# Seven products for eight in the Silu stages of a transformer block with a mixture of experts

## The chip, the cores and the metric

One core of one Trainium2 chip runs the whole kernel in fp32. The metric is the time of one execution on the device, in microseconds (us). TensorE (PE) multiplies, with its weight loads shown apart (PEld); VectorE (DVE), ScalarE (ACT) and GpSimd (POOL) do the elementwise work; SyncE (SP) mostly issues DMAs.

## The reference

x has 16 batches of 512 tokens with 256 features. It is normalized, and three terms are added to it: linear attention, a shared expert, and routed experts (two of eight a token, from one of two groups).

```python
xn = layernorm(x)                                   # no scale, no shift
# attention: q, k = elu(xn @ W + b) + 1; kv = k^T v per head; out = (q kv) / (q sum(k)) @ Wo + bo
# shared expert, HIDDEN = 512:
a, b = split(xn @ w_in.T, 2)                        # 256 -> 2 * 512
shared = (silu(a) * b) @ w_out.T
# routed experts share the first layer:
a, b = split(xn @ w1.T, 2)
h = silu(a) * b
routed = sum(h * weight[:, e] @ w2[e].T for e in range(8))   # two of the weights are not zero
out = x + attention + shared + routed
```

Each Silu stage, w1 for the routed experts and w_in for the shared one, is thus a product of 512 tokens x 256 features by 256 x 1024 for every batch.

## The kernel before, in words

The kernel is written in a framework that orders the instructions of each engine itself: a planner takes them by their place in the program and by the times it expects, so an engine's order may differ from the program's, except where `keep_in_program_order` or `issue_after` bind it. On the chip each engine then takes its instructions in that fixed order and waits on semaphores. The framework also assigns the buffers of a pool: `ps_mm` has six PSUM buffers of one bank (128 x 512 fp32), shared by everything with the tag "mm"; `ps_y` has two.

The first part loops over the 16 batches. Iteration b does, in program order:

- `front(b + 1)`: `residual` (POOL, x plus bias into `res`), `project` (PE: `pk`, `pq`; DVE and ACT: feature maps with Exp, tiles `km`, `qm`), `route` (many small DVE operations; `wins` and `ahead_of` on POOL).
- `summarize(b)`: PE `pxk`, an ACT copy to `xk`.
- `normalize(b + 2)`: DVE statistics, an ACT Sqrt (`sd`), DVE scaling to `xn`; `xn` goes to DRAM and comes back in blocks that DVE transposes into `xnT`, features on partitions, tokens along the free axis. Its statistics and Sqrt run ahead of the program's place when x has landed. `load_x(b + 3)` follows.
- `hidden_rows(b)`: the w1 stage. For each of four tiles of 128 tokens it multiplies the tokens (stationary) by the two halves of w1 (moving, 512 columns each), over two chunks of 128 features: 16 matmuls into eight PSUM tiles `phr`. ACT makes Silu of the first half (`sa_hr`), DVE multiplies it by the second (`hr`), SP stores the rows to `h_d` in DRAM.
- `key_sum(b + 1)` (POOL, one PE product `pks`) and `attend(b + 1)` (DVE operations on 1024 elements; SP stores and reloads q).
- `hidden(b)`: the w_in stage, transposed: weights are stationary, 512 tokens move. Four blocks of hidden features, two halves, two chunks: 16 matmuls into `phs`, then Silu and product into `hs_all`.
- `mix(b)` (PE `pvk`, DVE `vk`, PE `pm`, ACT copy `kvo`) and `gather(b)`: per token tile, four products of `hs_all` with `wout_sb` and two of `qT` with `kvo` (`po`, in `ps_y`), added to `res` and stored beside the h row in `h_d`.
- `load_expert`: two of the 16 slots of `w2_sb` an iteration, four DMAs of 128 KB each, on SP. All are loaded after eight batches.

In the last iteration hidden_rows comes first, and the steps of `order()` (the sorting of tokens by pair of experts) are placed between its tiles by `between`. Then the second part starts: for each pair of tiles, `rows()` gathers 2 x 128 rows of `h_d` by an indirect DMA on POOL, `turn()` transposes them (12 ACT copies `hb` and seven DVE transposes a pair; the first two pairs are placed behind instructions that `hidden` returns in `made`), `sums()` multiplies by the two experts of the pair, picked by a register offset into `w2_sb` (`py`), scales, adds, and stores by an indirect DMA.

[...]

Of the kernel before, what the change touches and what calls it, by code (L numbers as in the profile page):

```python
# [10 lines left out]
FP = mybir.dt.float32  # L11
AF = mybir.ActivationFunctionType
ALU = mybir.AluOpType
AX = mybir.AxisListType

P = 128
# [5 lines left out]
def block_kernel(  # L22
# [111 lines left out]
    KR = D + E + G  # L134
    wkr_sb = wp.tile([P, KD, KR], FP)
    nc.scalar.dma_start(out=wkr_sb[:, :, 0:D], in_=wk.rearrange("(p c) f -> p c f", p=P))
# [17 lines left out]
    if B > 1:  # L154
        xs[1] = load_x(1)
    w1_sb = wp.tile([P, KD, 2 * HID], FP)
    nc.sync.dma_start(out=w1_sb, in_=w1.rearrange("(p c) f -> p c f", p=P))
    win_sb = wp.tile([P, KD, 2 * HID], FP)
    nc.sync.dma_start(out=win_sb, in_=w_in.rearrange("(p c) f -> p c f", p=P))
    wv_sb = wp.tile([P, KD, D], FP)  # L160
# [11 lines left out]
    nc.sync.dma_start(out=wout_sb, in_=w_out.rearrange("(c p) d -> p c d", p=P))  # L172
    w2_sb = wp.tile([P, KH, G * NL * D], FP)

# [250 lines left out]
    def hidden_rows(b, xnT, then):  # L425

        for t in range(NT):
            halves = []
            for half in range(2):
                ph = ps_mm.tile([P, HID], FP, tag="mm", name=f"phr_{b}_{t}_{half}")  # L430
                for k in range(KD):
                    nc.tensor.matmul(  # L432
                        ph, lhsT=xnT[:, k, ts(t, P)], rhs=w1_sb[:, k, ts(half, HID)],
                        start=(k == 0), stop=(k == KD - 1),
                    )
                halves.append(ph)
            sa = work.tile([P, HID], FP, tag="sa", name=f"sa_hr_{b}_{t}")
            nc.scalar.activation(sa, halves[0], AF.Silu)  # L438
            hr = work.tile([P, HID], FP, tag="hr", name=f"hr_{b}_{t}", bufs=3)
            nc.vector.tensor_tensor(hr, halves[1], sa, ALU.mult)  # L440
            nc.sync.dma_start(out=h_d[ts(b * NT + t, P), 0:HID], in_=hr)
            between(b, then(t))

    def hidden(b, xnT):

        h = hs_all
        made = []
        for f in range(KH):
            halves = []
            for half in range(2):  # L450
                ph = ps_mm.tile([P, S], FP, tag="mm", name=f"phs_{b}_{f}_{half}")
                for k in range(KD):
                    nc.tensor.matmul(  # L453
                        ph, lhsT=win_sb[:, k, ts(half * KH + f, P)], rhs=xnT[:, k, :],
                        start=(k == 0), stop=(k == KD - 1),
                    )
                halves.append(ph)
            sa = work.tile([P, S], FP, tag="sa", name=f"sa_hs_{b}_{f}")
            made.append((
                nc.scalar.activation(sa, halves[0], AF.Silu),  # L460
                nc.vector.tensor_tensor(h[:, f, :], halves[1], sa, ALU.mult),  # L461
            ))
        return h, made
# [315 lines left out]
    fronts = {0: front(0, normed[0][1])}  # L779
    normed[1] = normalize(1)  # L780
    queries = {}
    xs[2] = load_x(2)
    for b in range(B):
# [22 lines left out]
        if b + 1 < B:  # L806
            hidden_rows(b, xnT, {2: 1}.get)
        ksb, (qT, turned) = sums, queries.pop(b)
# [6 lines left out]
        if b + 1 == B:  # L815
            for w in tiles[:AHEAD]:
                w.rows()
        hs, made = hidden(b, xnT)
        kvo = mix(b, xk, ksb)
# [39 lines left out]
    for half, queue in enumerate((nc.sync, nc.scalar)):  # L859
        far = work.tile([P, 2, D], FP, tag="hr", name=f"far_{half}", bufs=3)  # L860
        queue.dma_start(
# [40 lines left out]
```

## Time and profile before

| | |
|---|---|
| median of 3 runs | 1073.27 us (1071.79 to 1078.44) |
| profiled execution, its own time | 1071.43 us |
| its span, first to last instruction | 1069.6 us |
| granted TensorE clock | 1.000 |
| period of a middle batch | 50.77 us |
| first product of the routed part (`py`) starts at | 823.24 us |
| PE, DVE, ACT, POOL busy | 1052.6, 658.6, 375.7, 239.0 us |

A line of a group reads: line of the kernel, engine, operation, output and inputs by the program's names, shapes, count | busy us, mean ns of one | idle us of that engine just before them, and what ended the idle time. A line of a timeline has start and length in us, then engine, line and operation, and in square brackets the idle time ahead of it with what ended it. The durations of successive matmuls overlap, so their pitch is read from the start of one group to the start of the next.

### The profile page before, as it was taken

The page shows a single profiled execution, that of the slowest core. Times are in us where ns is not written, and L with a number is a line of the kernel's source. Part 1 is how long each engine was busy: PE and PEld are TensorE (multiplying, and loading weights), DVE is VectorE, ACT ScalarE, POOL GpSimd, SP SyncE. Part 2 cuts the span into 40 slices and gives each one's busy share as a digit, 9 for nine tenths or more (in the row PEclk, how much of TensorE's full clock was granted, in tenths as well). Part 3 has the DMA queues.
Part 4 walks back from the last instruction along what each step waited for, and adds up shares of the span by engine and source line. Part 5 has one row for each costly group of instructions (what it writes and reads, how often), then busy time and mean ns, then how long its engine had stood idle before and what let it go on. Part 6 is the DMA issues. An engine that isn't in the chain of part 4 may idle for free. (4 is left out here: it accounts for less than half of the span.)

```text
span 1069.6 us, 11317 instructions
## 1 busy us (share of the span) xinstructions
PE 1052.6 (98%) x3404; PEld 626.0 (59%) x3404; DVE 658.6 (62%) x1744; ACT 375.7 (35%) x703; POOL 239.0 (22%) x307
## 2 busy tenths in 40 slices
PE   7999999999999999999999999999999999999997
PEld 5574847475756666575757484757464444444445
DVE  6957466564647474747474655646864666666662
ACT  3413232223222231313131322212106676677760
POOL 6102111020202020201011110102003555555551
PEclk9999999999999999999999999999999999999999
DMA  7343342423324242423232313031213444554531
GB/s 232 99 119 119 80 137 60 138 81 117 116 88 139 66 135 68 139 60 99 70 108 60 117 42 119 21 117 39 81 50 128 137 151 148 155 152 146 155 123 64
DMA packets 129118, 114.18 MB, mean 107 GB/s; under 512 B 72045, under 2 KB 114045, under 8 KB 128800
## 3 DMA queue, kind: packets, MB, share of 16 engines
q1 hardware_dynamic: 119104, 77.16, 24.0%
q0 software_dynamic: 8976, 35.22, 10.8%
q10 hardware_dynamic: 976, 1.05, 0.3%
q8 instruction: 29, 0.48, 0.2%
q14 instruction: 33, 0.27, 0.1%
HBM read 63.52 MB, written 50.27 MB: 106 GB/s over the span
## 5 line engine op out<-in xcount | busy, mean ns | idle before, releaser
L747 PE MATMUL py<-w_sb,hT 128*128 x536 | 230.3, 592 | 0.2 <-ACT hb L718 0.2
L432 PE MATMUL phr<-w_sb,xnT 128*128 128x512 f32 x512 | 223.3, 593 | 0.0
L453 PE MATMUL phs<-xnT,win_sb 128*128 128x512 f32 x512 | 222.3, 592 | 0.0
L747 PEld LDWEIGHTS py<-w_sb,hT 128*128 128x128 f32 x536 | 101.8, 190 | 128.3 <-issue 127.7
L453 PEld LDWEIGHTS phs<-xnT,win_sb 128*128 128x128 f32 x512 | 97.3, 190 | 115.6 <-issue 112.2
L432 PEld LDWEIGHTS phr<-w_sb,xnT 128*128 128x128 f32 x512 | 96.9, 190 | 113.7 <-issue 105.2
L294 POOL TENSOR_TENSOR res<-x_all,bo_sb 128x1024 f32<-128x1024 f32 x16 | 38.8, 2428 | 435.3 <-DMA h_d<-res 324.0
L547 PE MATMUL po<-wout_sb,hs_all 128*128 128x256 f32 x512 | 123.4, 379 | 1.9 <-DVEq L845 1.9
L547 PEld LDWEIGHTS po<-wout_sb,hs_all 128*128 128x128 f32 x512 | 96.0, 190 | 15.1 <-issue 2.7
L461 DVE TENSOR_TENSOR hs_all<-phs,sa_hs 128x512 f32<-128x512 f32 x64 | 43.4, 681 | 93.5 <-PE phs L453 82.3
L556 DVE TENSOR_TENSOR res<-po,res 128x256 f32<-128x256 f32 x60 | 25.5, 424 | 116.4 <-PE po L547 116.4
L460 ACT ACTIVATE sa_hs<-phs 128x512 f32<-128x512 f32 x64 | 38.2, 597 | 147.9 <-PE phs L453 138.2
L760 POOL DMA_INDIRECT out<-y,goal x67 | 67.8, 1012 | 97.6 <-DVE y L757 87.6
L440 DVE TENSOR_TENSOR hr<-phr,sa_hr 128x512 f32<-128x512 f32 x64 | 43.8, 684 | 58.0 <-PE phr L432 32.7
L303 ACT ACTIVATE km<-km 128x1024 f32<-128x1024 f32 x16 | 16.9, 1057 | 175.4 <-DVE km L302 175.4
L438 ACT ACTIVATE sa_hr<-phr 128x512 f32<-128x512 f32 x64 | 38.0, 597 | 112.2 <-PE phr L432 103.5
L547 PE MATMUL po<-kvo,qT 128*128 128x256 f32 x256 | 66.8, 383 | 0.0
L314 PE MATMUL pk<-wkr_sb,xnT 128*128 128x266 f32 x256 | 61.6, 394 | 0.0
L481 PE MATMUL pxk<-kk_all,xn_all 128*128 128x256 f32 x256 | 57.9, 379 | 0.0
L325 PE MATMUL pq<-wq_sb,xnT 128*128 128x256 f32 x256 | 57.8, 379 | 0.0
L468 POOL TENSOR_TENSOR k<-kk_all 128x512 f32<-128x512 f32 x16 | 27.6, 1722 | 123.6 <-DVE sm L360 122.2
L314 PEld LDWEIGHTS pk<-wkr_sb,xnT 128*128 128x128 f32 x256 | 49.5, 194 | 9.0
(155 smaller groups left out, 1255.1 us busy)
## 6 DMA issues: line engine op xcount, KB each, us to landing
h_d<-hr SPq DMA_DIRECT2D x64, 256.0 KB, 2.5
q_d<-qq_all SPq DMA_DIRECT2D x16, 512.0 KB, 2.8
qb<-q_d SPq DMA_DIRECT2D x64, 128.0 KB, 2.6
w_sb<-in_w SPq DMA_DIRECT2D x64, 128.0 KB, 3.6
h_d<-res SPq DMA_DIRECT2D x60, 129.0 KB, 2.0
x_all<-in_x SPq DMA_DIRECT2D x15, 512.0 KB, 4.1
xn_d<-xn_all SPq DMA_DIRECT2D x14, 512.0 KB, 3.1
xb<-xn_d SPq DMA_DIRECT2D x56, 128.0 KB, 3.1
```

The costliest lines, as they stand in the source:

```text
L294: nc.gpsimd.tensor_tensor(res[:, :, 0:D], xs.pop(b), bo_sb.unsqueeze(1).to_broadcast([P, NT, D]), ALU.add)
L314: nc.tensor.matmul(pk, lhsT=xnT[:, k, ts(t, P)], rhs=wkr_sb[:, k, :], start=(k == 0), stop=(k == KD - 1),)
L325: nc.tensor.matmul(pq[:, t, :], lhsT=xnT[:, k, ts(t2 + t, P)], rhs=wq_sb[:, k, :], start=(k == 0), stop=(k == KD - 1),)
L432: nc.tensor.matmul(ph, lhsT=xnT[:, k, ts(t, P)], rhs=w1_sb[:, k, ts(half, HID)], start=(k == 0), stop=(k == KD - 1),)
L440: nc.vector.tensor_tensor(hr, halves[1], sa, ALU.mult)
L453: nc.tensor.matmul(ph, lhsT=win_sb[:, k, ts(half * KH + f, P)], rhs=xnT[:, k, :], start=(k == 0), stop=(k == KD - 1),)
L460: nc.scalar.activation(sa, halves[0], AF.Silu),
L461: nc.vector.tensor_tensor(h[:, f, :], halves[1], sa, ALU.mult),
L481: nc.tensor.matmul(pxk[:, c, :], lhsT=xn[:, t, ts(c, P)], rhs=kk[:, t, :], start=(t == 0), stop=(t == NT - 1),)
L547: nc.tensor.matmul(po, lhsT=a, rhs=w, start=(i == 0), stop=(i == len(parts) - 1))
L747: nc.tensor.matmul(py.rearrange("p j d -> p (j d)"), lhsT=self.hT[:, f, ts(j, P)], rhs=w2_sb[:, f, bass.ds(regs[i % TR], 2 * D)], start=(f ...
L760: stored = nc.gpsimd.indirect_dma_start(out=out_rows, out_offset=bass.IndirectOffsetOnAxis(ap=self.goal[:, i : i + 1], axis=0), in_=y, in_ ...
```

## The change

Both Silu stages are rewritten. Tokens and weights are cut in two each, as are the 256 features: x11, x12, x21, x22 (half m of the tokens, half k of the features) and w11, w12, w21, w22. The four blocks of the result, each a sum of two products before, come from seven products of sums of blocks (Winograd's form of Strassen's product). Four sums of token blocks are made per batch on POOL (`token_sums`, shared by both stages), and four differences of weight blocks once per weight on POOL (`weight_sums`).

`seven` runs the products in an order written out by hand, for two units u (two tiles of 128 tokens in `hidden_rows`, two pairs of feature blocks in `hidden`). A unit has three PSUM tiles. In `tall` the sums grow: M1, then M1 + M6, then M1 + M6 + M7, then M4 onto it; ACT copies the first three out between (r1, r2, b2), and DVE adds `lone` (M2) or `wide` (M5, then M3 onto it) to the copies. The results are Silu(r1) times r2 for the first half of the tokens, and Silu of the finished `tall` times b2 for the second. A product is one matmul of 512 columns in `hidden_rows` and two of 256 in `hidden`.

Beside it: the w1 blocks and wq lie in four expert slots of `w2_sb` (12 to 15), which are loaded only after the last `hidden_rows`; w1 and w_in come in three DMAs each; `hr` has four buffers for three; the first turns of the routed part hang on `made[0]` and `made[1]`, the second halves of the two units, for `made[1]` and `made[3]` before; the steps of `order()` in the last batch come after products 3, 6, 10 and 13.

```diff
+    def spare(i, n=1):
+        first = (LATE + 2 * (i % 2)) * D
+        return w2_sb[:, i // 2, first : first + n * HID]
...
-    wq_sb = wp.tile([P, KD, D], FP)
+    wq_sb = spare(7).rearrange("p (c f) -> p c f", c=KD)
...
+    w1_in = [spare(i) for i in range(SEVEN)]
+    win_sb = wp.tile([P, SEVEN, HID], FP)
+    win_in = [win_sb[:, i, :] for i in range(SEVEN)]
...
+        nc.sync.dma_start(out=left, in_=rows[:, :, 0:HID])
+        nc.sync.dma_start(out=corner, in_=rows[:, 0, HID:])
+        nc.sync.dma_start(out=blocks[2], in_=rows[:, 1, HID:])
...
+    def weight_sums(blocks, w12):
+        w11, w21, w22, t1, t2, t3, t4 = blocks
+        for to, p, m in ((t1, w12, w11), (t2, w22, t1), (t3, w22, w12), (t4, w21, t2)):
+            nc.gpsimd.tensor_tensor(to, p, m, ALU.subtract)
+    def token_sums(b, xnT):
+        x11, x12, x21, x22 = (xnT[:, k, ts(m, S // 2)] for m in range(2) for k in range(KD))
+        ss = one.tile([P, 4, S // 2], FP, tag="ss", name=f"ss_{b}")
+        s1, s2, s3, s4 = (ss[:, i, :] for i in range(4))
+        nc.gpsimd.tensor_tensor(s1, x21, x22, ALU.add)
+        nc.gpsimd.tensor_tensor(s2, s1, x11, ALU.subtract)
+        nc.gpsimd.tensor_tensor(s3, x11, x21, ALU.subtract)
+        nc.gpsimd.tensor_tensor(s4, x12, s2, ALU.subtract)
+        return [x11, x12, s4, x22, s1, s2, s3]
+    def seven(b, name, product, first, second, room, done):
...
+        for n, (u, i) in enumerate((
+            (0, 1), (0, 5), (0, 6), (1, 1), (0, 7), (1, 5), (1, 6), (0, 2), (1, 7), (0, 3), (0, 4),
+            (1, 2), (1, 3), (1, 4),
+        )):
+            to = lone[u] if i == 2 else wide[u] if i in (3, 5) else tall[u]
+            product(to, u, i - 1, i in (1, 2, 5), i in (2, 3, 4))
+            if i == 1:
+                r1[u] = work.tile([P, HID], FP, tag="sa", name=f"r1_{names[u]}")
+                nc.scalar.copy(r1[u], tall[u])
+            elif i == 6:
+                r2[u] = room(u, 0)
+                nc.scalar.copy(r2[u], first(tall[u]))
+            elif i == 7:
+                b2[u] = room(u, 1)
+                nc.scalar.copy(b2[u], first(tall[u]))
+                nc.vector.tensor_tensor(b2[u], b2[u], first(wide[u]), ALU.add)
+            elif i == 2:
+                nc.vector.tensor_tensor(r1[u], r1[u], lone[u], ALU.add)
+                nc.scalar.activation(r1[u], r1[u], AF.Silu)
+            elif i == 3:
+                nc.vector.tensor_tensor(r2[u], r2[u], first(wide[u]), ALU.add)
+                done(u, 0, None, nc.vector.tensor_tensor(r2[u], first(r1[u]), r2[u], ALU.mult))
+            elif i == 4:
+                sa = work.tile([P, HID], FP, tag="sa", name=f"sa_{names[u]}")
+                silu = nc.scalar.activation(sa, tall[u], AF.Silu)
+                done(u, 1, silu, nc.vector.tensor_tensor(b2[u], first(sa), b2[u], ALU.mult))
+            second(n)
...
+            nc.tensor.matmul(to, lhsT=xs7[i][:, ts(u, P)], rhs=w1_in[W7[i]], start=start, stop=stop, skip_group_check=True)
...
+            for f in range(2):
+                tc.keep_in_program_order(nc.tensor.matmul(
+                    split(to)[:, f, :], lhsT=win_in[W7[i]][:, ts(2 * u + f, P)], rhs=xs7[i],
+                    start=start and f == 0, stop=stop, skip_group_check=True,
+                ))
...
     normed[1] = normalize(1)
+    weight_sums(w1_in, w1_12)
...
         if b + 1 == B:
-            hidden_rows(b, xnT, dict.fromkeys(range(NT), 2).get)
+            sums7 = token_sums(b, xnT)
+            hidden_rows(b, sums7, {3: 2, 6: 2, 10: 2, 13: 2}.get)
+            for e in waiting:
+                load_expert(e)
...
+            weight_sums(win_in, win_12)
...
-            hidden_rows(b, xnT, {2: 1}.get)
+            sums7 = token_sums(b, xnT)
+            hidden_rows(b, sums7, {9: 1}.get)
...
-        for e in waiting[: 2 if b + 1 < B else G * NL]:
-            load_expert(e)
-        waiting = waiting[2:]
+        for e in [e for e in waiting[:2] if e < LATE]:
+            load_expert(waiting.pop(0))
...
-        w.turn(made[2 * i + 1])
+        w.turn(made[i])
```

More of the change, by code (lines that the diff above doesn't have):

```diff
@@ L135, in block_kernel @@
     wkr_sb = wp.tile([P, KD, KR], FP)
+    w2_sb = wp.tile([P, KH, G * NL * D], FP)
+    LATE = G * NL - 4
+    def spare(i, n=1):
+        first = (LATE + 2 * (i % 2)) * D
+        return w2_sb[:, i // 2, first : first + n * HID]
     nc.scalar.dma_start(out=wkr_sb[:, :, 0:D], in_=wk.rearrange("(p c) f -> p c f", p=P))
@@ L155, in block_kernel @@
         xs[1] = load_x(1)
[L156 to L159, printed above, removed]
+    SEVEN = 7
+    w1_in = [spare(i) for i in range(SEVEN)]
+    win_sb = wp.tile([P, SEVEN, HID], FP)
+    win_in = [win_sb[:, i, :] for i in range(SEVEN)]
+    w1_12, win_12 = (w2_sb[:, i, 0:HID] for i in range(2))
+    for w, left, blocks, corner in (
+        (w1, spare(0, 2).rearrange("p (c f) -> p c f", c=KD), w1_in, w1_12),
+        (w_in, win_sb[:, 0:KD, :], win_in, win_12),
+    ):
+        rows = w.rearrange("(p c) f -> p c f", p=P)
+        nc.sync.dma_start(out=left, in_=rows[:, :, 0:HID])
+        nc.sync.dma_start(out=corner, in_=rows[:, 0, HID:])
+        nc.sync.dma_start(out=blocks[2], in_=rows[:, 1, HID:])
     wv_sb = wp.tile([P, KD, D], FP)
@@ L172, in block_kernel @@
     nc.sync.dma_start(out=wout_sb, in_=w_out.rearrange("(c p) d -> p c d", p=P))
-    w2_sb = wp.tile([P, KH, G * NL * D], FP)
     def load_expert(i):
@@ L423, in between @@
                 next(steps_of_order)
[L425 to L442, printed above, removed]
@@ L444, in hidden @@
-    def hidden(b, xnT):
+    def weight_sums(blocks, w12):
[11 more added lines that the diff above has]
+        return [x11, x12, s4, x22, s1, s2, s3]
@@ new lines, in seven @@
+    def seven(b, name, product, first, second, room, done):
+        names = [f"{name}_{b}_{u}" for u in range(2)]
+        tall, lone, wide = (
+            [ps_mm.tile([P, HID], FP, tag="mm", name=f"{n}{i}") for n in names] for i in "abc"
+        )
+        r1, r2, b2 = [None] * 2, [None] * 2, [None] * 2
+        for n, (u, i) in enumerate((
[25 more added lines that the diff above has]
+            second(n)
@@ new lines, in hidden_rows, with product, room, done @@
+    def hidden_rows(b, xs7, then):
+        rows = {}
+        def product(to, u, i, start, stop):
+            nc.tensor.matmul(to, lhsT=xs7[i][:, ts(u, P)], rhs=w1_in[W7[i]], start=start, stop=stop, skip_group_check=True)
+        def room(u, half):
+            rows[u, half] = work.tile([P, HID], FP, tag="hr", name=f"hr_{b}_{u}_{half}", bufs=4)
+            return rows[u, half]
+        def done(u, half, silu, product):
+            nc.sync.dma_start(out=h_d[ts(b * NT + 2 * half + u, P), 0:HID], in_=rows[u, half])
+        seven(b, "phr", product, lambda a: a, lambda n: between(b, then(n)), room, done)
@@ L446, in hidden, with split, product, room @@
+    W7 = (0, 1, 2, 6, 3, 4, 5)
+    def hidden(b, xs7):
         h = hs_all
         made = []
[L448 to L462, printed above, removed]
+        def split(a):
+            return a.rearrange("p (f j) -> p f j", f=2)
+        def product(to, u, i, start, stop):
+            for f in range(2):
[3 more added lines that the diff above has]
+                ))
+        def room(u, half):
+            return h[:, 2 * u : 2 * u + 2, ts(half, S // 2)]
+        def done(u, half, silu, product):
+            if half:
+                made.append((silu, product))
+        seven(b, "phs", product, split, lambda n: None, room, done)
@@ L817, in block_kernel @@
                 w.rows()
-        hs, made = hidden(b, xnT)
+        hs, made = hidden(b, sums7)
         kvo = mix(b, xk, ksb)
@@ L859, in block_kernel @@
     for half, queue in enumerate((nc.sync, nc.scalar)):
-        far = work.tile([P, 2, D], FP, tag="hr", name=f"far_{half}", bufs=3)
+        far = work.tile([P, 2, D], FP, tag="hr", name=f"far_{half}", bufs=4)
         queue.dma_start(
```

## The prediction, made before the changed kernel was run

> **What bounds the kernel now.** I read the page first (engine shares, then groups), then the PE timeline of one batch, then busy time by window, then ScalarE, VectorE and GpSimd in the stretches that the change touches.
>
> ```profile
> span 1069.6 us, 11317 instructions
> ...
> PE 1052.6 (98%) x3404; PEld 626.0 (59%) x3404; DVE 658.6 (62%) x1744; ACT 375.7 (35%) x703; POOL 239.0 (22%) x307
> ...
> L432 PE MATMUL phr<-w_sb,xnT 128*128 128x512 f32 x512 | 223.3, 593 | 0.0
> ...
> L453 PE MATMUL phs<-xnT,win_sb 128*128 128x512 f32 x512 | 222.3, 592 | 0.0
> ...
> L440 DVE TENSOR_TENSOR hr<-phr,sa_hr 128x512 f32<-128x512 f32 x64 | 43.8, 684 | 58.0 <-PE phr L432 32.7
> ```
>
> TensorE is busy 98% of the span, and its two groups of Silu products show no idle time ahead of them (last column 0.0). Each group has 512 records, not the 256 matmuls of the program: an fp32 matmul is recorded as two passes. The PE timeline of a middle batch gives the pitch of a pass:
>
> ```profile
> 328.06 3.62 PE L325 MATMUL pq<-wq_sb,xnT 128*128 128x256 f32 x16
> 331.51 3.62 PE L481 MATMUL pxk<-kk_all,xn_all 128*128 128x256 f32 x16
> 334.96 13.90 PE L432 MATMUL phr<-w_sb,xnT 128*128 128x512 f32 x32
> 348.70 0.59 PE L471 MATMUL pks<-k,ones 128*128 128x256 f32 x2
> ```
>
> 32 passes of 512 columns take 348.70 - 334.96 = 13.74 us, 0.429 each, so a 512-column product of the program costs 0.86 us. 16 passes of 256 columns take 331.51 - 328.06 = 3.45 us, 0.2156 each. No bracket with idle time stands behind these rows. The windows show a whole batch, pk to pk:
>
> ```profile
> 324.46:375.23 50.77, 50.77 (x176) 32.26 (x174) 30.21 (x82) 13.50 (x18) 5.95 (x8) 1.00 0.36 104
> ```
>
> Columns: window, length, then busy us of PE, PEld, DVE, ACT, POOL, granted clock, DMA share, GB/s. PE fills all 50.77 us; DVE 30.2, ACT 13.5 and POOL 6.0 have room. So in the fifteen full batches each pass saved is time saved, as long as nothing new makes PE wait. The routed tail (from 823 us, py) is PE-bound too and is not changed.
>
> [...]beside the key sum (485.97 to 487.72) a 4-element VectorE operation takes 1.10 us, and its twin right after it 0.15:
>
> ```profile
> 485.97 1.75 POOL L468 TENSOR_TENSOR k<-kk_all 128x512 f32<-128x512 f32 x1 [4.20 <-DVE sm L360]
> ...
> 486.64 1.10 DVE L366 TENSOR_TENSOR gm<-ex 128x4 f32<-128x4 f32 x1
> 487.67 0.15 DVE L367 TENSOR_TENSOR gm<-ex 128x4 f32<-128x4 f32 x1
> ```
>
> **Passes removed.** hidden_rows: 16 matmuls (32 passes of 512) become 7 x 2 = 14 (28 passes): 13.74 - 28 x 0.4293 = 1.72 us. hidden: 32 passes of 512 become 7 x 2 x 2 matmuls of 256 columns, 56 passes: 13.74 - 56 x 0.2156 = 1.67 us. LDWEIGHTS takes 0.190 and stays below 0.2156, as in pq. Sum 3.38 us a batch, 54.1 us in 16 batches. Against the profiled execution's own 1071.43 us (span 1069.6 and 1.8 around it) that leaves 1017.3 if everything added is hidden. The median of the runs shown, 1073.27, is 0.2% above that execution; I leave this inside the range.
>
> **Work added on the other engines, per batch.** ScalarE: 3 copies per half, 12 in the two stages, at 0.57 (xk, 128x512 from PSUM): 6.8 us, 13.5 becomes 20.3. VectorE: 3 additions per half, 12 x 0.68 (the hr row) = 8.2 us, 30.2 becomes 38.4, 81% of a batch of 47.4. GpSimd: 4 token sums of 128x256 at 0.73 (second key sum): 2.9 us, 6.0 becomes 8.9. No engine becomes the bound by sum; what counts is order.
>
> **The chain inside seven().** M1 is copied out, M6 is added onto it in the same bank, the sum is copied, M7 is added. From the end of a product's pitch: its result is there 0.16 later (592 - 429 ns), ScalarE starts 0.08 after that (Silu at 787.25, passes done at 787.17), copies 0.57, and PE follows about 0.05 later (pm at 821.88 after vk at 821.83): 0.86 us, exactly the one product that is put between. So with ScalarE free the chains of half 0 cost about nothing. The second tight place is product (1,3), which needs b2 of half 1 copied and added: 0.24 + 0.57 + 0.08 + 0.68 + 0.05 = 1.62 us under three products (2.58), but Silu of r1 (0.60) stands ahead of that copy on ScalarE, and the addition and product for r2 of half 0 (2 x 0.68) beside its addition on VectorE. Slack is then below 0.4 us. Before, a pair of products took 3.4 us and used two of the six PSUM buffers, so two more pairs could run ahead of a late reader; now six tiles live at once in the six.
>
> What meets this chain is ScalarE's table changes, from the middle of the rows stage of batch 9:
>
> ```profile
> 487.65 0.57 ACT L486 COPY xk<-pxk 128x512 f32<-128x512 f32 x1
> 488.24 1.28 ACT L438 ACT_TABLE_LOAD   x1
> ...
> 493.22 1.28 ACT L269 ACT_TABLE_LOAD   x1
> 495.09 0.30 ACT L269 ACTIVATE sd<-mv,eps_sb 128x4 f32<-128x4 f32 x1 [0.59 <-DVE mv L267]
> 496.08 1.28 ACT L438 ACT_TABLE_LOAD   x1 [0.69 <-PE phr L432]
> ```
>
> Today the Sqrt of a later batch lies in a gap and blocks ScalarE in order: 1.28 + 0.59 + 0.30 + 1.28 = 3.45 us. Copies need no table, but they queue behind the loads, and PE queues behind the copies. Bounds: 0 if Sqrt falls after b2 of half 1, about 3 us if it falls between two chain copies. Its place is the planner's; I take 0.8 a batch. For VectorE's bursts (attend's operations of 1.2 us at the start of hidden, statistics in the rows stage) against the r2/b2 additions: 0 to 1.2, I take 0.4. Hand-over to the next stage (a PSUM buffer is freed only by the last Silu, 0.16 + 0.08 + 0.60 after the last product, with the 0.43 us key-sum product as cover; then gather waits for the late h of half 1): 0 to 0.9, I take 0.2. Sum 1.4 us x 15 = 21 us.
>
> **One-time edits.** Start: eight weight differences of 128x512 on GpSimd at 1.75 are 14 us; its idle stretches (13.8 to 17.2, 25.4 to 29.1, 35 to 44.8 us) hold most. But VectorE runs without a gap from 25 to 57 us in batch 0, and the additions join that line; if they came last, PE would wait all 8.2 us. Bounds 0 and 10; I take 6. The four late experts wait until the last product of hidden_rows(15) has read w1 in their place: 16 DMAs behind the last row store on SP at 0.41 each are 6.6 us of issue, and 3.6 to 4.6 to land: 11 us, 13 if their 2 MB share the queues with the tile gathers (233 GB/s there). pxk, hidden and mix cover 3.5 + 12.1 + 4; nothing is lost, 4 us if bandwidth fails. The first tile's turn now stands behind the Silu of product (0,4), 9.5 us into hidden instead of 5.4, so its 12 copies (5 us) end near 16.5 where PE is ready at 16: 1 us. Marks of the order on VectorE in the last rows stage: 1 us. End: 2 us. The finer loads of w1 and w_in add four DMA issues of 0.4 us on SP well ahead of their use at 30 us: nothing. wq's new place, four hr buffers: nothing.
>
> **Forecast:** 1017.3 + 21 + 6 + 2 = 1046 us.
>
> **Rivals.**
> The chain hides nearly whole (0.22): the planner sets Sqrt outside the tight places. For it: the order of products is fitted to 0.86 us, and ACT is idle 60% of the time. Against: it must hold 32 times. 1017.3 + 4 at the start + 0.2 x 15 = 1024.
> The 256-column halves run slower than I count (0.06): the page's po row has 123.4/512 = 0.241 a pass. Then 56 x 0.025 x 16 = 23 us come back: 1069. Against: pq and pxk show 0.2156 in a dense run.
> Slower (0.08): ScalarE's in-order queue becomes the bound inside both stages. If a table block of 3.45 us lands on the copy chain and VectorE's burst of 1.2 on the other stage's addition, it is 4.65 x 15 = 70, with 10 at the start and 3 at the end: 1017.3 + 83 = 1100. It decides from (54.1 - 8 + 10.7)/15 = 3.8 us of stall a batch on. Against: the block is that long only when the Sqrt waits for its statistics, and hidden has none where rows has it.
> The likeliest case (0.64) spans 1030 to 1064 by its bounds.
>
> **From these:** about 1% (10.7 us) is what a measurement of this kernel can tell from no change. Faster by more: 0.60 + 0.22 = 0.82; within: 0.04 of the likeliest and the 256-column case, 0.10; slower 0.08. The range 1022 to 1067 leaves out the slow case and part of the 256-column one.
>
> **What would show it.** phr 448 records at 0.43 and phs 896 at 0.216, no other group of PE changed; PE idle rows naming ScalarE copies or VectorE additions at the new products, 0.5 to 2.5 us a batch, most in rows stages with a Sqrt load in them; the batch period 48 to 49 us; routed products starting near 795 to 800 us. I am wrong if the period stays at 50.8, if the phs passes stretch beyond 0.22, if the routed tail first waits for a w2 DMA, or if batch 0 loses more than 10 us.

## The result, and the profile after

The kernel after takes 1079.18 us (median of 10 runs, 1078.17 to 1080.08), the kernel before 1075.30 (10 runs): a ratio of 1.0048, 95% interval 1.0029 to 1.0067. Half a per cent slower, where 1046 was forecast with 1067 as the upper end. The profiled execution took 1079.44 us. Executions of the kernel before range from 1069.9 us at a granted clock of 1.000 to 1078.8 at 0.995, and the profiled one (1071.43) is among the fastest, so the two spans lie 8.0 us apart where the medians lie 3.9 apart. Three lines of its page, then one middle batch by window (columns as before):

```profile
span 1077.6 us, 12384 instructions
...
PE 1025.4 (95%) x3724; PEld 682.5 (63%) x3724; DVE 791.3 (73%) x1936; ACT 470.0 (44%) x883; POOL 310.3 (29%) x379
...
L456 POOL TENSOR_TENSOR ss<-xnT 128x256 f32<-128x256 f32 x16 | 15.0, 937 | 269.0 <-PE phs_1c L534 269.0
```

```profile
233.47:282.21 48.74, 48.41 (x195) 35.40 (x194) 37.28 (x94) 19.08 (x29) 10.05 (x12) 1.00 0.38 109
```

The passes are gone as counted (phr 448 records, phs 896), yet TensorE is now busy 95% of the span, not 98%, and its busy time fell by 27 us only (records of 0.59 us overlap at a pitch of 0.43, so short waits under them count as busy, and so do passes at a halved clock, of which more below). The token sums' row gives the first hint: a sum of 128x256 takes 0.94 us in the mean (0.73 to 1.28), not 0.73, so something lengthens some of them. What TensorE waits for (columns: engine, line, releaser: us in total, times, longest us):

```profile
PE pm L595 <- DVE vk L590: 12.9, 9, 5.1
PE pt L302 <- DVE xn_all L292: 8.6, 2, 8.2
PE phs_0a L534 <- ACT r_phs L483: 6.3, 14, 2.3
PE pk L334 <- DVE qq_all L349: 4.0, 1, 4.0
PE phr_0a L508 <- ACT r_phr L483: 3.9, 1, 3.9
PE phr_1c L508 <- DVE hr L490: 3.2, 1, 3.2
PE phr_0c L508 <- DVE hr L490: 2.2, 5, 0.6
PE phs_1c L534 <- DVE hs_all L490: 1.7, 1, 1.7
```

Before, the same view had only pt (7.8), pm (3.5 in 2) and some 2 us of others. Every new row shown names a reader of the seven products or its neighbour on VectorE.

Where the 62 us went is read from the starts of the stages on TensorE (rows stage of batch b: first phr; routed part: first py). "Ideal" is before minus 3.38 us a batch:

| stretch | before | ideal | after | lost | forecast |
|---|---|---|---|---|---|
| up to rows(1) | 81.2 | 77.8 | 97.2 | 19.4 | 6 |
| rows(1) to rows(14), 13 batches | 659.9 | 616.0 | 645.3 | 29.3 (2.25 each) | 18.2 (1.4 each) |
| rows(14) to py, 2 batches | 82.2 | 75.4 | 87.1 | 11.7 | 4.8 |
| py to the end | 246.4 | 246.4 | 248.0 | 1.6 | 0 |

The losses add up to 62.0 us; 54.1 were saved; the difference is, to 0.1, the 8.0 us between the two spans. The periods are not even: 48.74 us in batches 2 to 6, 53.4 in batch 7, 49.8 to 50.1 in batches 8 to 12; the ideal is 47.38.

**The start.** GpSimd's row and VectorE's beside it:

```profile
17.76 2.37 POOL L314 TENSOR_TENSOR res<-x_all,bo_sb 128x1024 f32<-128x1024 f32 x1
...
21.77 2.34 POOL L314 TENSOR_TENSOR res<-x_all,bo_sb 128x1024 f32<-128x1024 f32 x1
```

```profile
17.84 2.84 DVE L322 TENSOR_SCALAR km<-kk_all 128x1024 f32<-128x1024 f32 x1
...
21.78 2.35 DVE L374 TENSOR_TENSOR ex<-lg,mx 128x8 f32<-128x8 f32 x1
```

km took 0.69 in the kernel before, the 8-element ex 0.16. Now ex ends with the GpSimd instruction beside it (24.13 and 24.11), and km ends 0.55 us behind its own neighbour (20.68 and 20.13), which is less than its 0.69. The author's estimate from these ends is that both waited for the neighbour, rather than ran slowly beside it; by what mechanism was not shown. The residual additions were there before; with the weight differences and token sums GpSimd is busy from 13.9 to 36.5 us without a gap, so VectorE, itself without a gap, loses time again and again: from 28.3 to 35.7 us gm takes 1.10 us, pe 0.72, and four operations of `beats` and `wins` 0.58 to 1.28, where 0.15 to 0.19 is what each takes elsewhere. rows(0) then starts at 37.6 (before 30.5), and lasts longer. Its first copy stands on ScalarE behind a late Exp (ScalarE, then TensorE):

```profile
42.99 1.06 ACT L323 ACTIVATE qm<-qm 128x1024 f32<-128x1024 f32 x1 [3.22 <-DVE qm L322]
43.95 0.22 ACT L378 ACTIVATE ex<-ex 128x40 f32<-128x40 f32 x1
44.08 0.57 ACT L483 COPY r_phr<-phr_0a 128x512 f32<-128x512 f32 x1
```

```profile
44.70 1.26 PE L508 MATMUL phr_0a<-w_sb,ss 128*128 128x512 f32 x2 [3.93 <-ACT r_phr L483]
45.75 1.92 PE L508 MATMUL phr_1c<-w_sb,ss 128*128 128x512 f32 x2
47.45 1.78 PE L508 MATMUL phr_0a<-w_sb,ss 128*128 128x512 f32 x2
```

Bracket: TensorE waits 3.93 us for that copy. The next two products have a pitch of 1.70 and 1.62 us for 0.86. The windows (columns as before) show the granted clock at one half there, and again where the routed part starts:

```profile
45.56:48.97 3.41, 3.41 (x5) 1.33 (x4) 3.41 (x11) 0.58 (x1) 0.00 (x0) 0.50 0.00 0
...
827.21:834.04 6.83, 5.20 (x9) 1.94 (x8) 3.95 (x11) 6.59 (x17) 0.00 (x0) 0.50 0.05 17
```

Three more such stretches of 3.41 us start at 25.08, 62.62 and 776.01. All five come behind waits of TensorE of 2.3 to 5.1 us; in the kernel before none lies between 12 and 1069 us. TensorE was busy for 18.6 of their 20.5 us, so by an estimate from these windows (half of that) up to 9 of the 62 us are lost to the halved clock.

**The end.** pm in batches 14 and 15, and the first routed product:

```profile
776.29 2.05 PE L595 MATMUL pm<-wo_sb,vk 128*128 128x256 f32 x4 [5.06 <-DVE vk L590]
...
826.58 1.43 PE L595 MATMUL pm<-wo_sb,vk 128*128 128x256 f32 x4 [3.69 <-DVE vk L590]
829.63 2.90 PE L831 MATMUL py<-w_sb,hT 128*128 x3 [1.63 <-DMA w_sb<-in_w]
```

Before, the two pm waited 1.82 and 1.71 us. The last row is the late experts' DMAs. The 1.6 us behind py are not this wait: the first 4.4 us of py run at half the clock, in the second of the windows above.

### The profile page after: what moved, and what is told of

Same layout as the page of the kernel before. It is cut to its first block, busy times and chain, and to the rows that moved or that the text cites. A ratio compares the mean times of both kernels' runs of the same rounds, so it can differ in the third digit from the quotient of the medians.

```text
span 1077.6 us, 12384 instructions
## 1 busy us (share of the span) xinstructions
PE 1025.4 (95%) x3724; PEld 682.5 (63%) x3724; DVE 791.3 (73%) x1936; ACT 470.0 (44%) x883; POOL 310.3 (29%) x379
## 5 line engine op out<-in xcount | busy, mean ns | idle before, releaser
L456 POOL TENSOR_TENSOR ss<-xnT 128x256 f32<-128x256 f32 x16 | 15.0, 937 | 269.0 <-PE phs_1c L534 269.0
L323 ACT ACTIVATE km<-km 128x1024 f32<-128x1024 f32 x16 | 16.9, 1058 | 171.5 <-DVE km L322 171.5
L334 PE MATMUL pk<-wkr_sb,xnT 128*128 128x266 f32 x256 | 65.0, 405 | 4.0 <-DVE qq_all L349 4.0
L345 PE MATMUL pq<-w_sb,xnT 128*128 128x256 f32 x256 | 57.8, 379 | 0.0
L631 PEld LDWEIGHTS po<-kvo,qT 128*128 128x128 f32 x256 | 47.5, 190 | 8.9 <-ACT kvo L599 3.0
L345 PEld LDWEIGHTS pq<-w_sb,xnT 128*128 128x128 f32 x256 | 48.6, 190 | 7.0
L565 PEld LDWEIGHTS pxk<-kk_all,xn_all 128*128 128x128 f32 x256 | 48.6, 190 | 6.6
L802 ACT COPY hb<-qq_all 32x256 f32<-32x256 f32 x108 | 43.4, 402 | 17.6 <-DMA qq_all<-h_d,source 12.3
L802 ACT COPY hb<-x_all 32x256 f32<-32x256 f32 (+1 forms) x108 | 42.1, 390 | 14.9 <-DVE hT L814 9.6
L802 ACT COPY hb<-xn_all 32x256 f32<-32x256 f32 x96 | 38.6, 402 | 15.8 <-DMA xn_all<-h_d,source 14.5
L802 ACT COPY hb<-kk_all 32x256 f32<-32x256 f32 x96 | 38.6, 402 | 14.5 <-DMA kk_all<-h_d,source 11.3
```

Source lines behind the costliest of these rows:

```text
L323: nc.scalar.activation(low, low, AF.Exp)
L334: nc.tensor.matmul(pk, lhsT=xnT[:, k, ts(t, P)], rhs=wkr_sb[:, k, :], start=(k == 0), stop=(k == KD - 1),)
L345: nc.tensor.matmul(pq[:, t, :], lhsT=xnT[:, k, ts(t2 + t, P)], rhs=wq_sb[:, k, :], start=(k == 0), stop=(k == KD - 1),)
L456: nc.gpsimd.tensor_tensor(s1, x21, x22, ALU.add)
L565: nc.tensor.matmul(pxk[:, c, :], lhsT=xn[:, t, ts(c, P)], rhs=kk[:, t, :], start=(t == 0), stop=(t == NT - 1),)
L631: nc.tensor.matmul(po, lhsT=a, rhs=w, start=(i == 0), stop=(i == len(parts) - 1))
```

## Experiments

Theory A: the reads of partial sums hold TensorE up, by ScalarE's copies and VectorE's additions. Rival B: what lies on GpSimd (sums and differences) does, through VectorE. Times are medians; "after" is 1079.18. Each kernel was timed beside the kernel before, whose median lay between 1075.3 and 1076.9 in these sessions, and the ratios are to that; a difference from after of less than about 2 us therefore says nothing. The first kernel takes every read away.

```diff
-  copies r1, r2, b2; additions of lone, wide
+  r1 = Silu(lone); r2 = wide * r1; b2 = Silu(tall) * r1
```

> Left out: the three copies and three additions of each half; Silu and the product act on the raw PSUM tiles, so the values are not the reference's. The seven products, token sums and weight differences stay. Theory A (the middle batches lose 1.7 to 2.7 of their 3.38 us to the reads of partial sums, through full ScalarE and VectorE queues): period of a middle batch 47.4 us, rows stage 12.0, hidden 12.1, no stall at pm in batch 14; batch 0 still begins its rows stage near 37.5 us, since the weight differences stay; total 1030 to 1042. Rival B (the loss sits in the hand-over between stages and in the six PSUM tiles, which stay): period above 48.2, total above 1058.

1041.66 us, ratio to before 0.9702 (0.9661 to 0.9743); periods 47.4 to 47.7 (48.6 in batch 7, 48.2 in batch 11), rows(1) at 88.3. So 37.5 us hang on the reads, with the GpSimd work all there: 8.9 up to rows(1), 25.5 in the thirteen middle batches, 4.3 in the last two. A holds for the middle; but it does not say whether the reads cost by their work or by where they stand. At the end the expectation failed. With no addition of partial sums left, pm waits for vk in both last batches all the same:

```profile
738.86 2.04 PE L586 MATMUL pm<-wo_sb,vk 128*128 128x256 f32 x4 [4.71 <-DVE vk L581]
...
789.17 1.25 PE L586 MATMUL pm<-wo_sb,vk 128*128 128x256 f32 x4 [4.14 <-DVE vk L581]
```

From rows(14) to pm it takes 30.7 us, 31.2 before and 33.8 in the kernel after; from rows(15) to pm 35.7, 36.6 and 35.7. In batch 14 VectorE works without a marked gap in the 20 us ahead of vk in all three. So there vk sets the time, passes that TensorE saves ahead of it turn into waiting, and the reads cost 3.1 us in batch 14 and nothing up to pm in batch 15.

**Token sums and buffers.**

```diff
-  ss = the four token sums (GpSimd); return [x11, x12, s4, x22, s1, s2, s3]
+  return [x11, x12, x12, x22, x21, x22, x21]
```

> Left out: the four token sums a batch on GpSimd; raw halves of the tokens stand in their place, so the values are not the reference's. Theory A (they are hidden beside gather): 0 to 4 us below the changed kernel, all of it in batch 0. Rival B [...]: period of a middle batch 0.3 us or more shorter, total 6 us or more below.

1065.09 us (0.9923, 0.9895 to 0.9951), 14.1 less than after. The waits of pm for vk fall from 12.9 us in 9 to 7.8 in 2, so B also has a part. The same with four SBUF buffers under the tag "sa" (two before):

```diff
-  r1[u] = work.tile([P, HID], FP, tag="sa", ...)    # and sa
+  r1[u] = work.tile([P, HID], FP, tag="sa", ..., bufs=4)
```

> As e3, without token sums, and with four SBUF buffers instead of two for r1 and the second Silu, which share a tag. Theory A (the first copy of hidden waits for the last product of rows to free one of the two buffers, and the second Silu for the first product): the wait of 0.2 to 0.4 us before the second product group of hidden goes in every batch, 5 to 8 us below e3. Rival B (PSUM buffers or VectorE's lateness hold the same products): within 2 us of e3.

1058.67 us (0.9863, 0.9821 to 0.9904), 6.4 less again. phs_0a's wait falls from 6.3 us in 14 to at most 0.8. Both were then tried with nothing left out. First the sums are held behind a one-column GpSimd copy of `kvo` of the batch before:

```diff
   kvo = mix(b, xk, ksb)
+  ticks.append(nc.gpsimd.tensor_copy(tick, kvo[:, 0, 0:1]))
...
+  with tc.issue_after(ticks[-1].ins):
       token_sums(...)
```

> The kernel after with one edit: GpSimd's token sums of a batch wait for a small GpSimd copy that reads the mixed weights of the batch before, so that they no longer run beside VectorE's last additions of the shared hidden stage. Nothing is left out. Theory (they cost by where they lie, through the slower VectorE and the later vk): the wait of pm for vk falls from 12.9 us in all to 5 to 8, the middle period from 48.74 to 48.1 to 48.3, and the time to 1067 to 1073 us. Rival (they cost by what they are: the first product of a stage needs them, wherever they lie): PE waits for the token sums instead, the period stays at 48.6 to 48.8, and the time at 1077 to 1080 us.

1070.25 us (0.9961, 0.9946 to 0.9976), 8.9 less; periods of 48.25 in batches 2 to 6, pm's waits 7.8 in 2. What they cost in the kernel after shows where GpSimd and VectorE meet at the end of hidden:

```profile
269.55 1.17 POOL L458 TENSOR_TENSOR ss<-xnT 128x256 f32<-128x256 f32 x1
```

```profile
270.06 1.21 DVE L496 TENSOR_TENSOR hs_all<-r_phs,hs_all 128x512 f32<-128x512 f32 x1
```

L496 takes 0.69 elsewhere. `ss` has one buffer, so the sums can start only when hidden's last product that reads it is done, and that is beside VectorE's last burst; vk comes after that burst, pm after vk. The same kernel once more:

> Once more the kernel with the token sums held, one look (1070.25 us before), to see whether its periods of 48.25 in batches 2 to 6, the 53.4 of batch 7 and the 49.2 after it come again. Theory (the order of issue is fixed in the program): they come again within 0.1 us. Rival (they are a state of the chip): they differ.

The periods came again: 48.25, then 53.4, then 49.2. They belong to the program. Then three buffers under "sa" (the pair sums of the keys share a buffer with `kvo` to make room):

```diff
-  r1[u] = work.tile([P, HID], FP, tag="sa", ...)    # and sa
+  r1[u] = work.tile([P, HID], FP, tag="sa", ..., bufs=3)
...
-  k2 = one.tile([P, 2, D], FP, tag="k2", ...)
+  k2 = one.tile([P, 2, D], FP, tag="kvo", ...)
```

> The kernel after with one edit: the copies of the first partial sums have three SBUF buffers for two; the room comes from the pair sums of the keys, which share a buffer with the mixed weights. Nothing is left out. Theory (the first copy of a stage waits for a buffer that the last product of the stage before still reads): phs_0a's wait of 6.3 us in 14 falls to under 1.5, the middle period to 48.2 to 48.4, the time to 1072 to 1075 us. Rival (the wait moves to the next thing, PSUM's banks or VectorE's additions): the period stays within 0.1 of 48.74 and the time within 2 us of 1079.

1068.09 us (0.9937, 0.9921 to 0.9954), 11.1 less, more than expected; periods 48.11 in batches 2 to 6, 48.6 to 49.3 later. The first copy of hidden, in the kernel after and then with three buffers:

```profile
258.21 0.58 ACT L483 COPY r_phs<-phs_0a 128x512 f32<-128x512 f32 x1 [1.17 <-DVE hr L496]
```

```profile
253.21 0.59 ACT L483 COPY r_phs<-phs_0a 128x512 f32<-128x512 f32 x1 [0.84 <-PE phs_0a L534]
```

The copy had waited for VectorE (the last reader of its buffer); with a third buffer it waits only for its product.

**The start and the end.** The raw quarters of the weights are loaded in place of the eight differences:

```diff
+  for to, k in zip(blocks[3:], (0, 1, 0, 1)):
+      nc.sync.dma_start(out=to, in_=rows[:, k, HID:])
...
-  weight_sums(w1_in, w1_12)
-  weight_sums(win_in, win_12)
```

> Left out: the eight weight differences on GpSimd; four more DMAs a weight put raw quarters in their place, so the values are not the reference's. Theory A (at the start [...]every operation of the first front waits): rows of batch 0 begin at 30 to 32 us instead of 37.6, total 6 to 10 us below the changed kernel. Rival B (the start is lost to the copies queued behind Exp on ScalarE and to VectorE's own queue in batch 0): rows still begin by 32 or earlier but batch 0 ends as late, total at most 3 us lower; or rows begin near 37 and nothing changes.

1071.60 us (0.9976, 0.9962 to 0.9990): rows(0) at 34.7, later than expected, and rows(1) at 88.5, 8.7 us earlier. The differences are near half of the start's loss; the reads, with 8.9 us in the first run, are near the other half. Then eight products in batch 0, with the differences written after it in the program, away from VectorE's first work (`eight_rows` and `eight` are the loops of the kernel before):

```diff
-  hidden_rows(b, sums7, ...); hidden(b, sums7)
+  eight_rows(b, xnT, w1_12, ...); eight(b, xnT, win_12)     # b == 0
...
   gather(b, ...)
+  if b == 0: weight_sums(w1_in, w1_12); weight_sums(win_in, win_12)
```

> Batch 0 keeps the eight products of before; the weight differences come after batch 0's gather, and the first experts are loaded from batch 1 on. Theory A (19 us are lost at the start: [...]batch 0's own queues delay the copies): rows of batch 0 at 30 to 31 us, rows of batch 1 at 81 to 84 us instead of 97, total 11 to 16 us below the changed kernel. Rival B (the 14 us of GpSimd work and the added VectorE work only move into batch 1 and cost the same there): rows of batch 2 no earlier than 140 us (146.5 in the changed kernel), total at most 6 us lower.

1083.86 us (1.0075, 1.0049 to 1.0101), a miss: nothing bound the differences, so the planner placed them at 13.5 to 30 us all the same, and the periods of batches 4 to 7 were 50.1 to 51.2. Eight products in batches 14 and 15 (w12 remade from a difference), alone and then with the former:

```diff
+  if b == 14: nc.gpsimd.tensor_tensor(t1, t1, w11, ALU.add)     # for w1 and w_in
-  hidden_rows(b, sums7, ...); hidden(b, sums7)
+  eight_rows(b, xnT, w1_in[3], ...); eight(b, xnT, win_in[3])   # b >= 14
```

> Batches 14 and 15 use the eight products of before; w12 is made again on GpSimd as t1 + w11. The late experts stay where they are. Theory A (in batches 14 and 15 VectorE is full of the marks of the order, and its additions come late): from the rows stage of batch 14 to the first routed product 82 to 84 us instead of 87, total 3 to 6 us below the changed kernel. Rival B (the late loads of four experts and the gathers set the start of the routed part): the stretch stays at 86 or more and the first routed product waits for a DMA.

> e5 and e6 together: seven products in batches 1 to 13 alone. If start and end are separate losses the gains add: 14 to 22 us below the changed kernel, 1057 to 1065 us, about 10 to 18 below the kernel before. Rival: the start's and the end's work meets the middle and less than half of that remains.

1075.04 us (0.9995, 0.9978 to 1.0011), 4.1 less than after; rows(14) to py 85.0 for 87.1. At the end eight products are faster than seven. Both ends: 1082.16 (1.0069, 1.0046 to 1.0092), a miss too, since the misplaced start stays in it. These with three buffers and held token sums:

> e7, with three SBUF buffers instead of two for r1 and the second Silu (the key sum's tile shares kvo's), and the token sums on GpSimd held back until kvo of the batch before is there, so that they don't run beside VectorE's burst at the end of hidden. Theory A ([...]the first copy of hidden waits for a buffer): a middle batch takes 47.6 to 48.2 us instead of 48.7 to 49.9, total 10 to 18 us below e7. Rival B (the middle's loss is the reads' own work on VectorE): within 5 us of e7.

1060.64 us (0.9859, 0.9828 to 0.9889). Now the start of the first-batch run with the differences bound:

```diff
+  held = nc.gpsimd.tensor_copy(tick0, hs[:, KH - 1, 0:1])       # b == 0
+  with tc.issue_after(held.ins):
       weight_sums(w1_in, w1_12); weight_sums(win_in, win_12)
-  waiting = list(range(G * NL))
+  waiting = [*range(2, LATE), 0, 1, *range(LATE, G * NL)]
```

> The kernel after with eight products in batch 0, as in the run of the first batch's eight products before, but now the eight weight differences are held behind a GpSimd copy that reads the hidden rows of batch 0, so that they cannot be issued in the first 40 us; experts 2 and 3 are loaded in batch 0, experts 0 and 1 last, so that the pace of loads is that of the kernel after. Theory (the start is lost to the differences beside VectorE's work, plus the late copies of the first seven-product stage): the first rows start at 31 to 33 us (after 37.6, before 30.5), batch 1's at 82 to 85 (after 97.2), the periods from batch 2 on stay at 48.7, the differences cost batch 0 or 1 up to 3 us, and the kernel takes 1066 to 1071 us. Rival (what is late at the start comes from the loads and from token sums, or the differences cost as much wherever they lie): batch 2's rows start no earlier than 143 us (after 146.5), and the time is 1076 to 1080 us.

rows(0) at 32.4, rows(1) at 83.7, rows(2) at 134.9 (after 146.5): the start behaved as the theory said, 13.5 us were won by rows(1). Yet the time is 1080.67 (1.0073, 1.0047 to 1.0100), not 1066 to 1071: batches 1 to 6 now take 51.2 us each, batch 7 52.7, and by rows(8) all is lost again. Products and sizes are the same as in the kernel after; the order on VectorE is not. Batch 4, GpSimd, VectorE, TensorE:

```profile
238.56 2.40 POOL L314 TENSOR_TENSOR res<-x_all,bo_sb 128x1024 f32<-128x1024 f32 x1
```

```profile
238.67 2.33 DVE L399 TENSOR_TENSOR beats<-pe 128x24 f32<-128x24 f32 x1
...
246.40 0.68 DVE L490 TENSOR_TENSOR hr<-hr,phr_0c 128x512 f32<-128x512 f32 x1
```

```profile
247.22 1.10 PE L508 MATMUL phr_0c<-w_sb,ss 128*128 128x512 f32 x2 [1.69 <-DVE hr L490]
```

and the same addition and product in the kernel after, a batch with a period of 48.74:

```profile
250.97 0.67 DVE L490 TENSOR_TENSOR hr<-hr,phr_0c 128x512 f32<-128x512 f32 x1
```

```profile
252.01 1.02 PE L508 MATMUL phr_0c<-w_sb,ss 128*128 128x512 f32 x2
```

L490 reads the first wide sum (M5) out of its bank, before the product M3 may be added onto it. On VectorE it stands behind the routing chain of the next batch, 22 small instructions. In the kernel after, the copy that L490 needs ends 1.7 us before L490 starts; TensorE comes 1.04 us behind L490's start and has 0.3 us to spare. In this run GpSimd's residual addition began 0.1 us ahead of the chain's first instruction with two SBUF inputs, `beats`, which took 2.33 us, not 0.17; L490 comes 9.1 us behind the start of rows, not 7.0, and TensorE waits. (The q transpose, 1.23 us, stands ahead of L490 in both.) In the kernel after the same addition runs at 250.34, beside L490 and L492, which read PSUM: both keep their 0.67 us. (From batch 8 on, in the kernel after, the statistics of a later batch, 1.6 us, stand in that chain in place of the transpose, and L490 starts as early, at 6.9; but phr_0c comes one product earlier there, and waits 0.4.)

To test this the chain from `beats` on is held behind `vk` of the batch before, in that kernel and in the kernel after (`ranks` is the part of `route` from `pf` on, batches 1 to 13):

```diff
   kvo = mix(b, xk, ksb)
+  with tc.issue_after(vk_instruction.ins):
+      ranks(b + 1, ...)
```

> The run with held weight differences (1080.7 us) with one more edit: the ranks and marks of routing of the next batch (from beats on, some 25 small VectorE instructions and GpSimd's few) wait until VectorE has made vk of this batch, when VectorE has gaps; nothing is left out. Theory (TensorE's second use of the first wide bank waits for an addition that stands behind this chain on VectorE): the wait phr_0c for hr of 13.8 us in 12 goes to under 2, the periods of batches 1 to 7 fall from 51.2 to 48.5 to 49.2, and the time to 1060 to 1066 us. Rival (the loads of the experts or GpSimd's place set the 51.2): the periods stay above 50.5 and the time above 1076.

> The kernel after with one edit, the ranks and marks of routing held behind vk of the batch before. Theory: the period, 48.74 in batches 2 to 6 and 49.85 to 53.4 from batch 7 on, becomes 48.3 to 48.8 throughout, and the time 1065 to 1071 us; the start stays late (batch 1's rows at 94 to 98 us). Rival: the later batches are slow for another reason, the periods from batch 7 on stay near 49.9, the time within 3 us of 1079.

With held differences: the wait is gone, the periods of batches 1 to 6 are 48.7 to 49.2 for 51.2, as the theory said. But the time is 1074.17 (0.9993), not 1060 to 1066. What took its place:

```profile
PE phs_0a L540 <- ACT r_phs L489: 9.4, 13, 1.4
...
PE po L679 <- DVE res L688: 5.5, 1, 5.5
PE pm L643 <- DVE beats L405: 5.2, 8, 1.0
```

In batch 0 batch 1's chain now meets the weight differences, and seven instructions with two SBUF inputs in a row take 1.12 to 1.30 us each beside them (the next two of the same lines, behind the last difference, 0.18 and 0.17); the residual additions stand behind the chain, and batch 0 takes 59.9 us. GpSimd, then VectorE:

```profile
65.69 1.26 POOL L455 TENSOR_TENSOR win_sb<-win_sb 128x512 f32<-128x512 f32 x1
```

```profile
65.79 1.19 DVE L406 TENSOR_TENSOR wins<-wins,beats 128x16 f32<-128x16 f32 x1
```

From batch 8 on the periods are 50.3 us. In the kernel after: 1079.62 (1.0036, 1.0021 to 1.0051), no gain, a miss. Here too the later periods are 50.3: phs_0a waits 1.41 us a batch, because the first copy of hidden waits 1.86 for the last product of rows, which reads its buffer. Leaving batch 1's chain where it was:

> The run with routing held (1074.2 us), but batch 1's routing is not held, so that in batch 0 nothing on VectorE stands behind GpSimd's weight differences. Theory: batch 1's rows start at 81 to 84 us again (after 97.2, the run with routing held 89.9), the periods of batches 1 to 7 stay at 48.7 to 49.2, the later ones at 50.3, and the time is 1064 to 1069 us: the gain of the start and that of VectorE's queue add. Rival (each gain comes back elsewhere): 1072 us or more.

1073.87 us (0.9995, 0.9980 to 1.0010): po's wait is gone, rows(1) at 86.0, but periods of 49.3 to 50.0 and 50.3, and pm waits for the chain (6.8 us in 11): the rival was right on the sum. One reader moved alone makes way for the next.

**All together.** Eight products at both ends, three buffers, held token sums and differences; then with the chain held behind vk; then behind the second residual addition, from batch 2 on:

```diff
   added = nc.vector.tensor_tensor(res[:, t, 0:D], po, res[:, t, 0:D], ALU.add)
+  if t == 1: with tc.issue_after(added.ins): ranks(b + 1, ...)
```

> Eight products in batches 0, 14 and 15, seven in the thirteen between, three buffers for the copies, the token sums held behind the mixed weights of the batch before, and the weight differences held behind batch 0's hidden rows; nothing is left out. Theory: the start of the kernel before (batch 1's rows at 82 to 85 us), periods of 48.2 to 48.7 between, the end of the kernel before: 1050 to 1057 us, 4 to 10 below the version whose differences ran at the start (1060.6). Rival (the start was not the differences): 1059 to 1063 us.

> The best version so far (1058.6 us: eight products at both ends, three buffers, token sums and weight differences held) with the ranks and marks of routing held behind vk as well. Theory: phr_0c's wait for hr of 14.1 us in 12 goes, the periods of batches 1 to 13 are all 47.7 to 48.2, and the time is 1043 to 1050 us. Rival: something else on VectorE's queue takes the place of the chain, and the time is 1056 to 1060 us.

> The best version (eight products at both ends, three buffers, token sums and differences held) with the routing chain of batches 2 to 13 held behind the second of the residual additions of the batch before, batch 1's not held. Theory: batch 1's rows at 82 to 86 us, no wait of po for res over 0.5 us, periods of 47.7 to 48.6 between, 1043 to 1052 us. Rival: the chain delays the last residual additions and the first keys of the next batch, periods of 49 us or more, 1055 to 1062 us.

1058.57 us (0.9856, 0.9817 to 0.9895; phr_0c still waits for hr, 14.1 us in 12, periods 49.9, then 48.5), 1060.42 (0.9853, 0.9815 to 0.9891; batch 0 takes 59.0, and in 8 batches po waits 13.4 us for residual additions that stand behind the chain: the rival), and **1049.25 us, ratio 0.9764 (0.9729 to 0.9798)**, faster than both kernels. Its PE row, its waits, and a middle batch:

```profile
PE 1022.5 (98%) x3664; PEld 671.3 (64%) x3664; DVE 772.8 (74%) x1900; ACT 448.9 (43%) x848; POOL 291.3 (28%) x386
```

```profile
PE pt L302 <- DVE xn_all L292: 7.3, 2, 6.9
PE pm L649 <- DVE vk L644: 6.4, 3, 4.3
PE pk L334 <- DVE qq_all L349: 2.5, 1, 2.5
PE phr_1c L520 <- DVE hr L502: 2.1, 1, 2.1
PE po L685 <- DVEq L1007: 1.6, 1, 1.6
```

```profile
277.90:325.90 48.00, 48.00 (x195) 35.58 (x195) 38.95 (x95) 19.11 (x30) 8.96 (x14) 1.00 0.37 110
```

TensorE is full again, and none of the new waits comes back in each batch. Between the ends the period is 47.9 to 48.3 (52.0 in batch 7), with every copy and addition in it, against 47.4 to 47.7 with none (48.6 in batch 7). So the reads' work costs about 0.5 us a batch, near the eight pitches of 0.93 for 0.86.

From rows(1) to rows(14) it takes 628.4 us, 619.8 without reads and 645.3 in the kernel after: of the 25.5 us that the reads cost there, 16.9 were their place. At the start and the end their place was not tried; there this kernel makes eight products. Of the 43.9 us that thirteen batches save in passes, 26.1 are left. From rows(14) to py it still takes 2.5 us longer than before, with the same products. Batch 14 takes 44.2 us as before; all of it stands in batch 15: ScalarE waits 4.03 us with its copies of the first gathered rows, while the late experts' loads run (DMA share 1.04 from 782.0 to 788.5 us); the copies then run ahead of the last two Silus, and pm waits 4.26 us for vk, not 1.71. That the loads held the rows up was not tried apart.

## Why the prediction was wrong, by its own steps

- **Passes removed, 54.1 us:** right. 256-column passes show no stretch (four of phs in 0.86 us, 66.56 to 67.42); without reads the period fell by 3.1 to 3.3 us, of 3.38, in most batches. But "each pass saved is time saved" failed in batches 14 and 15 (below).
- **Work added per batch:** nearly right. VectorE 37.3 us in the window (38.4 forecast), ScalarE 19.1 (20.3), GpSimd 10.1 (8.9; its token sums took longer than the 0.73 us forecast, 0.87 to 1.09 in the mean by line).
- **The chain inside seven(), "about nothing" with ScalarE free:** nearly right. The pitch behind a copied bank is 0.93 us for 0.86, eight times a batch, and rows stages take 12.3 us for 12.0: 0.6 us a batch, some 9 in all, that stand at nothing in the sum.
- **Middle, 1.4 us a batch:** measured 2.25, from other terms. In batches 2 to 6 it was 1.36, as forecast in the sum, but by luck: no Sqrt stands in those stages (0.8 forecast), 0.6 are the pitches, 0.4 the wait for a buffer, 0.4 lie behind pvk. The 0.8 for Sqrt was the wrong place: the rows stages of batches 8 to 12, with a Sqrt in them, take 0.6 us longer, and 0.4 of it is phr_0c's wait for VectorE. (The table loads behind that forecast: in the trace of the kernel before 59 `ACT_TABLE_LOAD` of 1.283 us each, one ahead of ScalarE's first function and one at each change among Exp, Silu and Sqrt, none with the line of a copy.) The hand-over (0.2) looked at PSUM alone and missed that the copies share two SBUF buffers; a third won 11.1 us. VectorE's bursts (0.4) were counted against attend and the statistics, not against routing, whose chain stands ahead of L490 (0.4 us a batch from batch 8 on; 1.7 when the weight differences were moved). And the token sums were added as 2.9 us on an idle engine, though their one buffer sets their start at VectorE's busiest moment: 8.9 us, of which 7.5 in the middle.
- **Start, 6 with bounds 0 and 10:** measured 19.4, the largest error. The step "its idle stretches hold most" of the eight differences failed: they stood at nothing in the 6 us, and rows(1) came 8.7 us earlier without them. GpSimd had the time; VectorE, named in the next sentence as being without a gap, had none to spare for operations that ended only with a GpSimd neighbour (ex 2.35 us for 0.16). The prediction had shown a 4-element operation of 1.10 us beside the key sum, but put no price on it. The reads came to 8.9, where the additions, for which the 6 us were taken, had been bounded by 8.2; the late Exp before the first copy (3.93) was not foreseen, nor were three stretches at half the clock, up to 5.1 us of the 19.4.
- **End, 2 plus two batches:** forecast 4.8, measured 11.7. The step that failed is that 3.38 us are won in each of the last two batches. pm was already waiting for vk there (1.82 and 1.71 before), and without any read the two stretches up to pm were only 1.4 us shorter than before, so 5.4 of the 6.8 us saved became waiting. The marks of order(), taken as 1 us, and the additions meet on VectorE in batch 14: 3.1. The halved clock behind the longer wait of pm costs 1.6 (14.6 us from pm to rows(15) for 13.0, granted clock 0.50). The late experts, "nothing is lost", held the first py for 1.63 us. That is 11.7, as the table has it.
- **Slower by ScalarE's queue becoming the bound:** false in its mechanism; after the start, copies were late where VectorE or a buffer made them late. The losses together, 62 us, came near the 65 (54.1 + 10.7) from which the kernel would have been slower by 1%, by other ways. Two of the prediction's own signs of being wrong came true: the routed part first waits for an expert's DMA, and batch 0 loses more than 10 us.

In sum: 62 us lost for 29 forecast, 13 at the start, 11 in the middle, 7 at the end, 2 behind it. What stays open: why the planner's order changes at batch 7 (one wait of 3.2 us in the kernel after, 2.1 in the best), and what of the 62 us would be left without the halved clock, which follows the stalls and was not tried apart from them.

## What to carry to other kernels

Saved passes are worth their time only while each reader between them is on time, so look up, for every new copy or addition, what stands ahead of it in its engine's order, which buffer it needs and who read that last, in SBUF as well as in PSUM. Work put on an idle GpSimd was charged to VectorE here where both read SBUF (beside GpSimd's residual addition `beats` took 2.33 us for 0.17, while additions with an input in PSUM kept 0.67): place it (bind it with an order, not by its place in the program) where VectorE reads PSUM or has gaps. When single fixes bring less than their waits, make them together: moved one at a time, each wait here was followed by the next. And where TensorE already waits for another engine, as pm did in the last two batches, passes saved ahead of that wait are not time saved.

## What the runs showed of the hardware that was not expected

- A VectorE instruction of 8 or 24 elements a partition took 2.35 us (`ex`, kernel after) or 2.33 (`beats`, batch 4 of the run with the first eight held) when a GpSimd addition of 2.34 or 2.40 us had begun 0.01 or 0.11 us earlier, 0.16 or 0.17 with no GpSimd work beside it; additions with one input in PSUM (L490, L492 in the kernel after) kept 0.67 us beside the same GpSimd addition.
- After a TensorE wait of 3.93 us two products had pitches of 1.70 and 1.62 us for 0.86, and after one of 2.27 the next three together took 4.28 us for some 2.6; the granted clock was 0.50 for 3.41 us in both places, and for 6.83 us after waits of 3.69 and 1.63. The length of the wait alone did not decide it: one of 2.15 us in batch 7 of the best kernel was followed by it (the first product of hidden has a pitch of 1.71 us; granted clock 0.50 from 388.48 to 391.89), one of 3.21 us in batch 7 of the kernel after was not (1.00 from 405.5 to 408.0).
